# Row maxima and softmax denominators reach all partitions through DRAM instead of TensorE transposes, with exp four steps behind the scores

## The chip, the cores and the metric

The kernel runs on one NeuronCore of a Trainium2 chip. Its time is the device time of one execution in microseconds (us); lower is better. Five engines with instruction streams of their own matter here: TensorE (PE), VectorE (DVE), ScalarE (ACT), GpSimd (POOL) and SyncE (SP), which only issues DMAs. All five take their instructions in order, and wait on semaphores for each other.

## The reference

Four cross-attention layers run one after the other on `x` (2048 tokens, 256 channels), each with the same context (1601 rows of 512). Three layers are "masked" (16 heads of 64, a bias at a few keys from two masks), the second is "grouped" (16 query heads of 16 on 4 key heads, an RMS norm in front). All is float32. A masked layer, cut to what matters:

```python
q = (x @ Wq), k = (ctx @ Wk), v = (ctx @ Wv)          # 16 heads of 64
logits = einsum('bhqd,bhkd->bhqk', q, k) * 64 ** -0.5
logits = logits + col_bias                            # -20 * (1 - mask) at the token columns
probs = softmax(logits, axis=-1)                      # over 1601 keys
out = einsum('bhqk,bhkd->bhqd', probs, v)
x = x + out @ Wo + bo
```

The softmax of a query row needs the row's maximum before the exponential, and the row's sum afterwards.

## The kernel before, in words

Scores are kept transposed: keys on the 128 partitions, queries in the free dimension. A *unit* is two heads by 512 queries; a masked layer has 8 blocks (pairs of heads) by 4 query blocks, so 32 units, and there are 96 masked units and 32 grouped ones. The 1601 keys are 13 chunks of up to 128, so a unit has 13 *steps*. The main loop (L1067) runs over steps and overlaps three units in a software pipeline: at one step it makes the scores of chunk `ca` of one unit, the exponential of chunk `cb` of the unit before, `NT + DELAY` = 13 + 2 steps behind, and the product with V of the chunk one step (`LAG`) behind that.

A masked unit goes through these steps:

- `masked_scores` (L745): two matmuls into a PSUM buffer `s` (L751), ACT copies it to an SBUF chunk buffer `p` (L763), DVE keeps a running maximum `top` (L766, L768). The pool of `p` has `NP` = 17 buffers, that of `s` has two.
- `maxima` (L798), one step after the last chunk: eight TensorE transposes (L805) and a DVE reduction (L806) give the negative maximum `ntop`, one value per query, with the queries on the partitions.
- `maxima_spread` (L812), a step later: eight more transposes (L818) of a broadcast of `ntop` put the maxima on all partitions, in the PSUM buffer `b` named `less`.
- `subtract` (L831): DVE adds `less` to the chunk in place (L834). Then `exp` (L836): ACT takes the exponential in place (L841), and POOL adds the chunk to the running `sums` (L844 for chunks 0 and 1 together, L846 for the rest).
- `values` (L862): TensorE accumulates the product with V in `po` (L869); after the last chunk ACT copies it to `oT`.
- `denominators` (L881): eight transposes of `sums` (L888), a DVE reduction (L889) and a reciprocal (L890) give `rden`; POOL copies it in a broadcast form to `by` (L899).
- `divide` (L904): four transposes of `by` (L907) put the reciprocals on the partitions of the output, and DVE multiplies them into `o` (L911). `project` (L913): two matmuls with Wo (L917), each added to `xs` by DVE (L923).

The grouped units compute the maxima in another layout and fold them into a second matmul (L850, L855), get their denominators from a row of ones (L894, L897), and use the same L899, L907 and `project`. POOL makes no sums for them.

Between the scores and the values of a step, the loop puts *pieces* of other work into TensorE's stream: the projections of K (L369) and V (L384) for the next block, the queries of the next unit (L420), and denominators, divide and project of the unit just done. `Pieces` (L970) hands them out by a credit per step; `urgent` pieces go ahead of `fill`. The context slices `ct` that the projections read are loaded from DRAM by SP (L204), in three buffers, asked for as a piece starts.

At the end (L1125 to L1131) the instructions of PE, ACT and DVE are tied to the order in which they were written; those of POOL and SP are ordered by the framework's scheduler.

## Time and profile before

| | |
|---|---|
| median of 3 runs | 5643.22 us (5641.31 to 5643.86) |
| profiled execution | 5653.54 us, span 5651.8 us |
| granted TensorE clock, mean | 0.98 |
| PE, DVE, ACT, POOL busy | 94%, 71%, 57%, 50% of the span |
| DMA | 252.88 MB, mean 45 GB/s |

How to read it: a line such as `L846 POOL TENSOR_TENSOR sums<-sums,p 128x1024 f32<-128x1024 f32 (+1 forms) x1056 | 2499.2, 2367 | 1097.9 <-ACT p L841 1084.8` is a group of instructions of source line 846 on POOL: what is written from what, the shapes (partitions by elements), the count; then the busy time in us and the mean of one in ns; then how long the engine sat idle just before them, and which engine's work ended that. In the timeline a row has its start in us, its length in us, the engine, the line and the tiles; a bracket gives the idle time before it. TensorE's fp32 matmuls appear as two records each.

### The profile page before, as it was taken

The page shows a single profiled execution, that of the slowest core. Times are in us where ns is not written, and L with a number is a line of the kernel's source. Part 1 is how long each engine was busy: PE and PEld are TensorE (multiplying, and loading weights), DVE is VectorE, ACT ScalarE, POOL GpSimd, SP SyncE. Part 2 cuts the span into 40 slices and gives each one's busy share as a digit, 9 for nine tenths or more (in the row PEclk, how much of TensorE's full clock was granted, in tenths as well). Part 3 has the DMA queues.
Part 4 walks back from the last instruction along what each step waited for, and adds up shares of the span by engine and source line. Part 5 has one row for each costly group of instructions (what it writes and reads, how often), then busy time and mean ns, then how long its engine had stood idle before and what let it go on. Part 6 is the DMA issues. An engine that isn't in the chain of part 4 may idle for free.

```text
span 5651.8 us, 59516 instructions
## 1 busy us (share of the span) xinstructions
PE 5321.4 (94%) x22444; PEld 1865.2 (33%) x22444; DVE 4013.6 (71%) x4140; ACT 3196.2 (57%) x3513; POOL 2837.7 (50%) x1380
## 2 busy tenths in 40 slices
PE   6999999998889999999999999999999999999997
PEld 3333333332323333233233333333333333333332
DVE  3777777777765555555567777777777777777786
ACT  2666666665433434333456666666666666666665
POOL 1766666665410000000056666666666666666676
PEclk8999999999889999999999999999999999999998
DMA  4112211111100000001012111212111121111100
GB/s 135 32 57 60 59 49 53 55 56 44 39 20 5 9 9 9 9 13 52 15 51 61 56 54 49 57 56 59 46 56 55 54 59 49 53 56 52 54 17 15
DMA packets 209744, 252.88 MB, mean 45 GB/s; under 512 B 43529, under 2 KB 155401, under 8 KB 209456
## 3 DMA queue, kind: packets, MB, share of 16 engines
q1 hardware_dynamic: 206192, 243.69, 14.8%
q8 instruction: 177, 2.90, 0.2%
q0 software_dynamic: 1152, 3.28, 0.2%
q10 hardware_dynamic: 2112, 2.10, 0.1%
q14 instruction: 111, 0.91, 0.1%
HBM read 235.27 MB, written 13.76 MB: 44 GB/s over the span
## 4 chain that ended last, share of the span: by engine, by line
PE 78%; ACT 7%; POOL 7%; DVE 5%; issue 2%; DMA 0%; SPq 0%; ACTq 0%; POOLq 0%; DVEq 0%
PE po L869 24%; PE s L751 20%; PE pm L384 6%; PE pm L369 5%; PE pm L917 5%; POOL sums L844 4%; ACT p L763 4%; ACT p L841 3%; POOL sums L846 3%; PE s L850 2%; PE s L784 2%; PE pm L420 2%; PE s L805 2%; PE b L818 2%; PE s L855 2%
## 5 line engine op out<-in xcount | busy, mean ns | idle before, releaser
L846 POOL TENSOR_TENSOR sums<-sums,p 128x1024 f32<-128x1024 f32 (+1 forms) x1056 | 2499.2, 2367 | 1097.9 <-ACT p L841 1084.8
L763 ACT COPY p<-s 128x1024 f32<-128x1024 f32 (+1 forms) x1248 | 1263.4, 1012 | 1434.0 <-PE s L751 1138.3
L869 PE MATMUL po<-p,v 128*64 128x512 f32 (+1 forms) x6656 | 1821.7, 626 | 36.5 <-ACT p L841 34.7
L768 DVE TENSOR_TENSOR top<-s,top 128x1024 f32<-128x1024 f32 (+1 forms) x1056 | 1291.5, 1223 | 753.9 <-ACT p L763 749.4
L751 PE MATMUL s<-q,kT 64*128 64x512 f32 (+1 forms) x4992 | 1426.3, 648 | 117.6 <-DVE top L768 116.4
L834 DVE TENSOR_TENSOR p<-p,b 128x1024 f32<-128x1024 f32 (+1 forms) x1248 | 1504.7, 1206 | 2.4 <-PE b L818 2.0
L841 ACT ACTIVATE p<-p 128x1024 f32<-128x1024 f32 (+1 forms) x1248 | 1321.5, 1059 | 110.3 <-DVE p L834 109.4
L869 PEld LDWEIGHTS po<-p,v 128*64 128x64 f32 (+1 forms) x6656 | 332.0, 136 | 1032.1 <-issue 698.9
L899 POOL COPY by<-rden 128x512 f32<-128x512 f32 x128 | 78.5, 613 | 1111.8 <-DVE rden L897 1083.9
L751 PEld LDWEIGHTS s<-q,kT 64*128 64x128 f32 (+1 forms) x4992 | 370.7, 182 | 732.7 <-issue 454.6
L859 ACT ACTIVATE p<-s 128x1024 f32<-128x1024 f32 (+1 forms) x283 | 289.8, 1024 | 451.0 <-PE s L855 450.9
L844 POOL TENSOR_TENSOR sums<-p 128x1024 f32<-128x1024 f32 x96 | 226.5, 2360 | 434.2 <-ACT p L841 434.2
L789 DVE TENSOR_REDUCE row_top<-s 128x2 f32<-128x1024 f32 x261 | 318.6, 1221 | 122.9 <-PE s L784 121.9
L384 PEld LDWEIGHTS pm<-wv,ct 128*128 128x128 f32 (+1 forms) x2392 | 284.7, 187 | 218.9 <-issue 215.9
L384 PE MATMUL pm<-wv,ct 128*128 128x128 f32 (+1 forms) x2392 | 337.6, 286 | 0.5 <-ACT v L389 0.5
L369 PE MATMUL pm<-ct,wk 128*128 128x512 f32 (+1 forms) x736 | 315.8, 544 | 2.7 <-ACT kT L374 2.7
L917 PE MATMUL pm<-o,wo 128*128 128x512 f32 x512 | 292.0, 653 | 7.1 <-DVE xs L923 2.9
L859 ACT ACTIVATE p<-b 128x1024 f32<-128x1024 f32 (+1 forms) x133 | 136.2, 1024 | 217.8 <-PE b L855 217.8
L923 DVE TENSOR_TENSOR xs<-pm,xs 128x512 f32<-128x512 f32 x232 | 158.4, 683 | 90.4 <-PE pm L917 90.4
L806 DVE TENSOR_REDUCE ntop<-s 128x8 f32<-128x1024 f32 x96 | 117.6, 1225 | 130.9 <-PE s L805 130.6
L789 DVE TENSOR_REDUCE row_top<-b 128x2 f32<-128x1024 f32 x123 | 150.2, 1221 | 62.2 <-PE b L784 61.6
L420 PE MATMUL pm<-xT,wq 128*128 128x512 f32 x336 | 188.5, 644 | 0.0
(191 smaller groups left out, 3279.2 us busy)
## 6 DMA issues: line engine op xcount, KB each, us to landing
ct<-ctxT SPq DMA_DIRECT2D x288, 512.0 KB, 3.8
xT<-xT SPq DMA_DIRECT2D x104, 512.0 KB, 3.5
ct<-ctxT SPq DMA_DIRECT2D x48, 130.0 KB, 2.6
wk<-in_L_xattn_Wk_dram SPq DMA_DIRECT2D x24, 256.0 KB, 4.4
wv<-in_L_xattn_Wv_dram SPq DMA_DIRECT2D x24, 256.0 KB, 3.1
xT<-xs SPq DMA_DIRECT2D x12, 512.0 KB, 2.6
wq<-in_L_xattn_Wq_dram SPq DMA_DIRECT2D x24, 128.0 KB, 2.1
wo<-in_L_xattn_Wo_dram SPq DMA_DIRECT2D x24, 128.0 KB, 2.1
```

The costliest lines, as they stand in the source:

```text
L369: nc.tensor.matmul(u.pk[:, :n], u.wk[:, k, :], ct(k, a, n), start=(k == 0), stop=(k == NCT - 1),)
L384: nc.tensor.matmul(u.pv[:m, c - c0, :], ct(k, a, m), u.wv[:, k, :], start=(k == 0), stop=(k == NCT - 1),)
L751: nc.tensor.matmul(s[:m, h, :], self.u.kT[r, a : a + m], self.q[r, :], start=True, stop=(a != TAIL),)
L763: nc.scalar.copy(p[:m], s[:m])
L768: nc.vector.tensor_tensor(self.top[:m], s[:m], self.top[:m], ALU.max)
L789: nc.vector.tensor_reduce(self.top[:, :, q, k : k + 1], s, AX.X, ALU.max)
L834: nc.vector.tensor_tensor(self.p[c][:m], self.p[c][:m], self.less[:m], ALU.add)
L841: nc.scalar.activation(p[:m], p[:m], AF.Exp)
L844: nc.gpsimd.tensor_tensor(self.sums, self.p[0], p, ALU.add)
L846: nc.gpsimd.tensor_tensor(self.sums[:m], self.sums[:m], p[:m], ALU.add)
L869: nc.tensor.matmul(self.po[r, :], u.v[:m, c, r], self.p[c][:m, h, :], start=(c == 0), stop=(c == NT - 1),)
L917: nc.tensor.matmul(py, wo[:, ts(k, P)], self.o, start=True, stop=True)
```

## The change

- `maxima` of a masked unit sends `ntop` (128 partitions, 8 values) to a DRAM tile `cols` by one DMA, and a second DMA reads it back to all 128 partitions (512 KB) as `less`, now an SBUF tile. A query's values lie four apart in it, so `subtract` reads `less` with a step of 16 bytes. `maxima_spread` with its eight transposes is gone for masked units.
- `denominators` sends `rden` the same way, and two DMAs of 64 partitions read it back as `by`. `divide` multiplies `by` into `oT` in place; the POOL copy and the four transposes are gone, for masked and grouped units.
- The PSUM buffer `b` is given up for a third `s`. `NP` is 19, `DELAY` is 4. `wk`, `wv` and `xT` have one buffer instead of two.
- POOL starts `sums` with a copy of chunk 0 instead of adding chunks 0 and 1.
- The queries of the next unit come due two steps later, denominators two steps after the last values, divide and project four steps after that. The credit is no longer at least one piece per step. `ct` loads are asked for after the piece that frees their buffer.

```diff
-    NP = 17
+    NP = 19
-    ps_s = ctx.enter_context(tc.tile_pool(name="ps_s", bufs=2, space=PSUM))
-    ps_b = ctx.enter_context(tc.tile_pool(name="ps_b", bufs=1, space=PSUM))
+    ps_s = ctx.enter_context(tc.tile_pool(name="ps_s", bufs=3, space=PSUM))
...
+    def on_all_partitions(cols, to):
+        rows = dram.tile([2, P, QT], FP, name="cols", bufs=4)
+        with nc.allow_non_contiguous_dma(reason="1024 values, four at a time"):
+            nc.sync.dma_start(out=rows.rearrange("h p q -> p h q"), in_=cols)
+        for tile_, heads_ in to:
+            src = rows[heads_].rearrange("(o h) p q -> o (h p q)", o=1)
+            nc.sync.dma_start(out=tile_, in_=src.to_broadcast(tile_.shape))
...
                 nc.vector.tensor_reduce(ntop, pt, AX.X, ALU.max, negate=True)
+                less = work.tile([P, 2, P, QT], FP, name="less")
+                on_all_partitions(ntop, [(less.rearrange("n h p q -> n (h p q)"), slice(0, 2))])
+                self.less = less.rearrange("n h p q -> n h q p")
...
-                self.less = ps_b.tile([P, 2, QB], FP, name="b")
-                for h in range(2):
-                    for q in range(QT):
-                        nc.tensor.transpose(
-                            self.less[:, h, ts(q, P)],
-                            self.ntop[:, h, q : q + 1].to_broadcast((P, P)), ident,
-                        )
...
         def subtract(self, c):
             if self.masked:
                 m = TCH[c][1]
-                nc.vector.tensor_tensor(self.p[c][:m], self.p[c][:m], self.less[:m], ALU.add)
+                p = self.p[c][:m].rearrange("n h (q p) -> n h q p", p=P)
+                nc.vector.tensor_tensor(p, p, self.less[:m], ALU.add)
...
-                if c == 1:
+                if c == 0:
                     self.sums = work.tile([P, 2, QB], FP, name="sums")
-                    nc.gpsimd.tensor_tensor(self.sums, self.p[0], p, ALU.add)
-                elif c:
+                    nc.gpsimd.tensor_copy(self.sums, p)
+                else:
                     nc.gpsimd.tensor_tensor(self.sums[:m], self.sums[:m], p[:m], ALU.add)
...
-            self.by = work.tile([P, QT, 2, 64], FP, name="by", bufs=1)
-            nc.gpsimd.tensor_copy(
-                self.by,
-                rden.rearrange("p h (q o) -> p q h o", o=1).to_broadcast((P, QT, 2, 64)),
+            by = work.tile([P, P, QT], FP, name="by", bufs=1)
+            on_all_partitions(
+                rden,
+                [(by[self.rows(h)].rearrange("r p q -> r (p q)"), slice(h, h + 1)) for h in range(2)],
             )
+            self.by = by.rearrange("r p q -> r q p")
 
         def divide(self):
-            pr = ps_m.tile([P, QB], FP, name="pm")
-            for q in range(QT):
-                nc.tensor.transpose(
-                    pr[:, ts(q, P)], self.by[:, q].rearrange("p h o -> p (h o)"), ident
-                )
-            self.o = work.tile([P, QB], FP, name="o", bufs=1)
-            nc.vector.tensor_tensor(self.o, pr, self.oT, ALU.mult)
+            oT = self.oT.rearrange("r (q p) -> r q p", p=P)
+            nc.vector.tensor_tensor(oT, oT, self.by, ALU.mult)
+            return True
...
-            self.credit = min(self.credit + share, 2.0)
+            self.credit = min(self.credit, 0.9) + share
...
-    DELAY, LAG = 2, 1
+    DELAY, LAG = 4, 1
...
         if valuing and cv == NT - 1:
-            pieces.urgent.extend(valuing.finish_groups())
-            pieces.urgent.extend(after(kv))
+            due.setdefault(step + 2, []).append([valuing.denominators])
+            due.setdefault(step + 6, []).extend(valuing.finish_groups() + after(kv))
+        pieces.urgent.extend(due.pop(step, ()))
...
-            steps = NT - ca + (NT - 2) * after_this
-            pieces.step(max(1.0, (pieces.left() + 6 * after_this) / steps))
+            steps = NT - ca + (NT - 1) * after_this
+            pieces.step((pieces.left() + 5 * after_this) / steps)
```

## The prediction

> **What bounds the kernel now.** I read the page first: busy time, the chain, the costliest groups.
>
> ```profile
> PE 5321.4 (94%) x22444; PEld 1865.2 (33%) x22444; DVE 4013.6 (71%) x4140; ACT 3196.2 (57%) x3513; POOL 2837.7 (50%) x1380
> ...
> PE 78%; ACT 7%; POOL 7%; DVE 5%; issue 2%; DMA 0%; SPq 0%; ACTq 0%; POOLq 0%; DVEq 0%
> ...
> L846 POOL TENSOR_TENSOR sums<-sums,p 128x1024 f32<-128x1024 f32 (+1 forms) x1056 | 2499.2, 2367 | 1097.9 <-ACT p L841 1084.8
> ...
> L834 DVE TENSOR_TENSOR p<-p,b 128x1024 f32<-128x1024 f32 (+1 forms) x1248 | 1504.7, 1206 | 2.4 <-PE b L818 2.0
> L841 ACT ACTIVATE p<-p 128x1024 f32<-128x1024 f32 (+1 forms) x1248 | 1321.5, 1059 | 110.3 <-DVE p L834 109.4
> ```
>
> TensorE sets the pace; POOL's half share hides that it works only in the masked layers, 2.37 us per chunk. The chain in order of time gives TensorE's true pitch; two records are transposes that the change removes:
>
> ```profile
> 4200.65 1.06 PE s L751 x4
> 4201.72 1.01 PE po L869 x4
> 4202.72 1.02 PE b L818 x8
> ...
> 4256.55 0.66 PE pm L907 x4
> ```
>
> A masked unit on TensorE: 13 steps of 1.06 + 1.01 = 26.9; three sets of eight transposes (L805, L818, L888), 3.1; L907 0.7; four 512-wide matmuls (L420, L917) at 1.06 = 4.2; the bias 0.4; a quarter of a block's projections, (12 x 1.06 + 1.04 + 13 x 1.09) / 4 = 7.0. Sum 42.2 us. The window 4200 to 5500 holds 30 maxima reductions (L806), so a unit takes 43.3: TensorE idles 1.1.
>
> The decisive view is the timeline where DVE has an instruction with both inputs in SBUF while POOL adds a chunk. That happens only between layers:
>
> ```profile
> L691 DVE SCALAR_TENSOR_TENSOR xT<-xs,normw,rest x32: 337/349/2514, 1438.2 to 1637.6; 128x128 f32<-128x128 f32 x32
> ```
> ```profile
> 1442.00 1.97 DVE L691 SCALAR_TENSOR_TENSOR xT<-xs,normw,rest 128x128 f32<-128x128 f32 x2
> ...
> 1449.98 0.61 DVE L691 SCALAR_TENSOR_TENSOR xT<-xs,normw,rest 128x128 f32<-128x128 f32 x2
> ```
> ```profile
> 1441.20 2.35 POOL L846 TENSOR_TENSOR sums<-sums,p 128x1024 f32<-128x1024 f32 x1 [3.44 <-ACT p L841]
> 1446.33 2.35 POOL L846 TENSOR_TENSOR sums<-sums,p 128x1024 f32<-128x1024 f32 x1 [2.77 <-ACT p L841]
> ```
>
> The pair at 1449.98, with no sum beside it, takes 0.61. The pair at 1442.00 takes 1.97: POOL's sum ends at 1443.55, and the pair ends 0.42 later. DVE stands still until POOL is done. L834 shows nothing of this today (always near 1206 ns): its second input `b` lies in PSUM.
>
> **What the change removes.** From TensorE, per masked unit 1.02 + 0.66 = 1.7 us, leaving 40.5; per grouped unit 0.66. From POOL the copy L899 (128 of 0.61). The wait of ACT for POOL's first sum, which comes of adding chunks 0 and 1 together, goes with the copy of chunk 0; what it cost is within the 1.1. Late next is not TensorE:
>
> **What it adds, 1: two engines on one port.** `less` moves to SBUF, so all 13 subtractions of a masked unit become what L691 is, beside a POOL that sums in the same steps. In series a unit needs 12 sums x 2.37 = 28.4, the copy of chunk 0 about 1.0 (L899 does half the elements in 0.61, the rest by POOL's other rows), 13 subtractions x 1.21 = 15.7, and a divide of 0.69, also two SBUF inputs now: 45.9. A blocked DVE instruction has its start behind it when the port comes free; the cast L523 ended 0.29 after POOL where alone it takes 0.42, so 0.13 is hidden, 1.7 a unit: 44.2. Were POOL's start hidden too, 42.5. The trace never shows DVE first and POOL waiting; the ends are 0 (they overlap) and 1.21 a chunk. I take the full exclusion, the nearest row being the exclusion seen from the other side.
>
> To reach 44.2 POOL must have a sum waiting whenever DVE lets go. `NP` 19 allows about two steps of lag (13 + 4 + 2). But DVE's stream puts other work between two subtractions: the denominators' reduction and reciprocal in one step, divide and a residual add in another. There POOL goes first, DVE loses its turn, and the port then waits for an exp (1.06 and some 0.17 of handoffs). Two such turns a unit: 2.4. Masked unit: 46.6, against 43.3: +3.3 x 96 = **+317 us**.
>
> **2: round trips in place of transposes.** A trip is a 4 KB write of 16-byte pieces and a read on all partitions. Rows for landing times:
>
> ```profile
> xT<-xT SPq DMA_DIRECT2D x104, 512.0 KB, 3.5
> ...
> wq<-in_L_xattn_Wq_dram SPq DMA_DIRECT2D x24, 128.0 KB, 2.1
> ...
> wo<-in_L_xattn_wo_dram SPq DMA_DIRECT2D x16, 16.0 KB, 1.7
> ...
> tok_idx<-ttn_token_indices_A_dram SPq DMA_DIRECT2D x3, 1.0 KB, 3.2
> ```
>
> The write lies between 1.7 and 3.2; I take 1.9, nearer the short row, as it spreads over all partitions. Reads of `by` are two of 128 KB in flight together, 2.1 (4.4 at worst, as wk's 256 KB). With 0.4 of issues and handoffs, 4.4 us, from 3.8 to 8.0.
>
> For `less` it is 1.9 + 3.5 + 0.4 = 5.8. In DVE's stream three subtractions and three maxima stand between the reduction and the first use, about 10 us: nothing, unless SP is held in front of it by a context load waiting for TensorE (such waits last up to 24 us today); then the subtraction waits, with every maximum behind it.
>
> For `by` there is less cover than the diff suggests. Divide comes due four steps after denominators, but the credit, no longer one per step, hands denominators out late and divide promptly. In the built program DVE has 3, 2 or 1 pairs of subtraction and maximum between reciprocal and divide in masked units (0 in three). At 3.4 us a pair only the last kind (21 units, 1.0 short) waits; it drains POOL's backlog meanwhile, so I charge nothing more; uncovered, it would be 0.2 a unit on average.
>
> Grouped units have no slack: their TensorE is 98% busy (1700 to 2650: 934.25 of 950). From the denominator matmuls to project: handoffs and reciprocal 0.4, trip 4.4, divide 0.69, handoffs 0.4, so 5.9. TensorE's stream holds between them nothing in nine units, 2.1 to 2.4 us in seventeen, 4.8 in three, 11 or more in three: 9 x 5.9 + 17 x 3.5 + 3 x 1.1 = 116 us of stall, less 32 x 0.66 of transposes, +95. A gap that long also costs clock:
>
> ```profile
> 1446.24 1.08 PE L869 MATMUL po<-p,v 128*64 128x512 f32 x4 [2.99 <-ACT p L841]
> ...
> 1452.87 1.98 PE L869 MATMUL po<-p,v 128*64 128x512 f32 x4 [3.31 <-ACT p L841]
> ```
>
> After 2.99 idle the four records take 1.08, after 3.31 idle 1.98, and it stays so until 1462.3: some 4.7 us lost. For the nine with the longest gap, +42. Together **+137**. With trips of 3.8 and no clock loss +75; with 8.0, and clock lost at 29 gaps, some +330.
>
> **3: the rest, at nothing.** The third `s` was there in grouped units as `b`; in masked ones it only lets scores run further ahead. Single `wk`, `wv`: their loads (4.4, 3.1 us) come after the last projection of a block, and SP's stream has them among the work of the last steps; the first projection that needs them comes a step or more later. If late, once per block: 24 x 4.4 = 105 at most. Moved `ct` loads go past `cols` in SP's stream in 22 of 128 denominators; the next piece bounds that. Some 85 MB more DMA on 253 MB at 15% of the queues: no bound. The last unit's trip at the end: +6.
>
> **The step of 16 bytes.** Here a row and a rule differ. `subtract` reads one element in four. The nearest row is a DVE copy read at a step of 64 bytes (L273), beside one without a step (L251):
>
> ```profile
> L273 DVE COPY max_cols<-p x8: 170/174/181, 91.5 to 98.0; 128x24 f32<-128x24 f32 x8
> ```
> ```profile
> L251 DVE COPY max_cols<-less x32: 174/174/176, 1586.3 to 2779.9; 128x8 f32<-128x8 f32 x32
> ```
>
> Twenty-four stepped elements take the same 174 ns as eight dense ones, so I take no loss. But the row is short. DVE's rows for 512 elements show two rates a factor apart, 0.42 us (L523) and 0.69 (L524), a start of 0.15 taken off: 1 to 2; one more halving is the other end, 13 x 1.07 + 0.53 = +14.4 a unit. The Trainium skill (Advanced Engine Details and Errata, Memory Cachelines) says that SBUF lines are 16 bytes and that at least two accesses to a line are needed to hide its latency; at this step each access meets a new line. By the row the total is the sum below; by the rule, taken as a halved rate, it would be about 7480 (an estimate).
>
> **Sum**, against the profiled execution of 5653.5 (span 5651.8): 5653.5 + 317 + 137 + 6 = 6114. It lies 10 above the median of the runs, so about **6100** in their terms.
>
> **Rivals.**
> - *The step halves the rate.* Subtraction 2.28: +14.4 x 96 = 1382 more, 7480. For: no row reads 1024 elements at a step. Against: L273.
> - *Lock step.* If POOL never has a sum waiting, a chunk is subtraction 1.08, exp 1.06, sum 2.37, handoffs 0.17: 4.7, a unit 13 x 4.7 - 1.3 + 0.7 = 60.5, and 7440 in all; half the steps so, about 6770. For: subtraction and exp feed the very sum that blocks the next subtraction. Against: after its maximum DVE asks for the port some 0.1 us before the exp is done.
> - *Faster: no exclusion* between this add and the sums, since `tensor_tensor` itself was never seen blocked. Then TensorE stays the bound: 40.5, plus its stall at project, where the chain from the denominators' transposes is 5.9 + 1.5 = 7.4 against covers of 8.5, 4.2, 5.3 and 2.1 in a block's four units: 2.6 on average. 43.1 a unit, -20, and the grouped 137: 5770. With a trip of 3.4 (two landings of 1.7) the stalls shrink to 1.8 and 2.8: (42.3 - 43.3) x 96 + 69 + 6 = -21, 5622. It decides from a trip below about 4.0. Against: L691 and L523 are blocked each time a sum runs.
>
> **How the numbers follow.** Exclusion with unit 44.2 to 48.5 and grouped +75 to +330: 0.48, 5810 to 6480, the forecast 6100. Lock step, partly or whole: 0.17. Halved rate: 0.15. No exclusion with the usual trip: 0.08, of which 0.03 within 0.2%. With the short trip, faster: 0.12. A measurement tells 0.2% (11 us) from no change. Faster 0.12, same 0.03, slower 0.85. The range 5660 to 7460 leaves out the faster cases and the upper end of the slowest.
>
> **What would show it.** Subtractions well over 1.21 us wherever a sum runs, ending just after it, or POOL's sums longer; a masked unit of 46 to 47; TensorE near 87% with the longest waits on DVE; in grouped units waits at project on the divide, the divide on a DMA, and a lower granted clock there. I am wrong if subtraction stays at 1.21 beside a sum of 2.37, or if it is 2.3 with no sum beside it.

## The result, and the profile after

The changed kernel takes **7425.75 us** (median of four runs, 7423.34 to 7426.9), the kernel before 5643.54 beside it (5641.31 to 5646.77). The ratio is 1.3157, with a 95% interval from 1.3134 to 1.318. The forecast was 6100: the direction was right and the time lies inside the stated range, 5660 to 7460, but near its upper end: the loss is 1782 us, where some 456 had been forecast.

From the page of the kernel after (span 7421.6): busy times, the chain that ended last, and four of the costliest groups.

```profile
PE 5643.3 (76%) x21164; PEld 1831.4 (25%) x21164; DVE 6154.7 (83%) x4140; ACT 3240.7 (44%) x3513; POOL 4540.9 (61%) x1348
...
DVE 35%; PE 29%; issue 28%; DMA 5%; ACT 1%; POOL 1%; SPq 0%; DVEq 0%; POOLq 0%; ACTq 0%
...
L855 POOL TENSOR_TENSOR sums<-sums,p 128x1024 f32<-128x1024 f32 (+1 forms) x1152 | 4241.1, 3682 | 1286.1 <-ACT p L850 1076.9
L843 DVE TENSOR_TENSOR p<-p,less 128x1024 f32<-128x1024 f32 (+1 forms) x1248 | 3569.3, 2861 | 2.4 <-DMA less<-cols 2.2
...
L923 PE MATMUL pm<-oT,wo 128*128 128x512 f32 x512 | 437.3, 949 | 666.5 <-DVE oT L916 602.9
...
L916 DVE TENSOR_TENSOR oT<-oT,by 128x512 f32<-128x512 f32 x128 | 239.0, 1867 | 173.7 <-DMA by<-cols 173.7
```

TensorE has 1280 matmul records fewer, and yet more busy time than before: its granted clock is 0.89, where it was 0.98. DVE is the busiest engine. Its subtraction has gone from 1.21 to 2.86 us, POOL's sum from 2.37 to 3.68. Both records hold waiting inside them, as the timeline of a masked stretch shows (start, length, engine, line; POOL's five sums are one row):

```profile
5017.63 18.88 POOL L855 TENSOR_TENSOR sums<-sums,p 128x1024 f32<-128x1024 f32 x5 [0.33 <-ACT p L850]
...
5020.50 3.10 DVE L843 TENSOR_TENSOR p<-p,less 128x1024 f32<-128x1024 f32 x1
...
5023.51 1.22 DVE L782 TENSOR_TENSOR top<-s,top 128x1024 f32<-128x1024 f32 x1
...
5024.64 3.05 DVE L843 TENSOR_TENSOR p<-p,less 128x1024 f32<-128x1024 f32 x1
...
5027.62 1.21 DVE L782 TENSOR_TENSOR top<-s,top 128x1024 f32<-128x1024 f32 x1
...
5028.75 3.11 DVE L843 TENSOR_TENSOR p<-p,less 128x1024 f32<-128x1024 f32 x1
...
5034.28 4.07 DVE L843 TENSOR_TENSOR p<-p,less 128x1024 f32<-128x1024 f32 x1
...
5041.19 1.64 DVE L916 TENSOR_TENSOR oT<-oT,by 128x512 f32<-128x512 f32 x1 [1.71 <-DMA by<-cols]
```

A subtraction follows a maximum every 4.1 us, while POOL's sums run without a pause. At 5034.28, after the denominators' reduction and reciprocal, DVE comes 0.11 us behind POOL's next sum (start 5034.17) and stands until it is over. At 5041.19 the divide has waited for its DMA.

Where did the 1782 us go? The start of the maxima's reduction on DVE marks the masked units. The mean distance of its 94 successive starts inside the masked layers is a masked unit; the one long distance spans the grouped layer. Before: 44.31 us and 1293.7. After: 60.16 and 1553.4. So 15.85 x 96 = 1522 lie in the masked units and 260 in the grouped stage: 1782.

### The profile page after: what moved, and what is told of

Same layout as the page of the kernel before. It is cut to its first block, busy times and chain, and to the rows that moved or that the text cites. A ratio compares the mean times of both kernels' runs of the same rounds, so it can differ in the third digit from the quotient of the medians.

```text
span 7421.6 us, 57991 instructions
## 1 busy us (share of the span) xinstructions
PE 5643.3 (76%) x21164; PEld 1831.4 (25%) x21164; DVE 6154.7 (83%) x4140; ACT 3240.7 (44%) x3513; POOL 4540.9 (61%) x1348
## 3 DMA queue, kind: packets, MB, share of 16 engines
q0 software_dynamic: 1152, 3.28, 0.1%
## 4 chain that ended last, share of the span: by engine, by line
DVE 35%; PE 29%; issue 28%; DMA 5%; ACT 1%; POOL 1%; SPq 0%; DVEq 0%; POOLq 0%; ACTq 0%
DVE top L782 14%; DVE p L843 12%; PE po L878 7%; PE pm L923 6%; PE s L765 4%; DVE oT L916 3%; DMA by<-cols 3%; PE s L798 3%; PE s L859 2%; DMA cols<-rden 2%; PE s L864 2%; PE pm L370 2%; DVE rden L898 1%; DVE top L780 1%; DVE ntop L820 1%
## 5 line engine op out<-in xcount | busy, mean ns | idle before, releaser
L855 POOL TENSOR_TENSOR sums<-sums,p 128x1024 f32<-128x1024 f32 (+1 forms) x1152 | 4241.1, 3682 | 1286.1 <-ACT p L850 1076.9
L843 DVE TENSOR_TENSOR p<-p,less 128x1024 f32<-128x1024 f32 (+1 forms) x1248 | 3569.3, 2861 | 2.4 <-DMA less<-cols 2.2
L878 PE MATMUL po<-p,v 128*64 128x512 f32 (+1 forms) x6656 | 1946.4, 665 | 1006.3 <-ACT p L850 890.0
L765 PE MATMUL s<-q,kT 64*128 64x512 f32 (+1 forms) x4992 | 1532.1, 693 | 0.7 <-DVE top L780 0.7
L923 PE MATMUL pm<-oT,wo 128*128 128x512 f32 x512 | 437.3, 949 | 666.5 <-DVE oT L916 602.9
L868 ACT ACTIVATE p<-s 128x1024 f32<-128x1024 f32 (+1 forms) x416 | 425.6, 1023 | 882.6 <-PE s L864 881.9
L853 POOL COPY sums<-p 128x1024 f32<-128x1024 f32 x96 | 267.2, 2784 | 735.5 <-ACT p L850 735.5
L803 DVE TENSOR_REDUCE row_top<-s 128x2 f32<-128x1024 f32 x384 | 469.0, 1224 | 218.6 <-PE s L798 215.1
L916 DVE TENSOR_TENSOR oT<-oT,by 128x512 f32<-128x512 f32 x128 | 239.0, 1867 | 173.7 <-DMA by<-cols 173.7
L859 PE MATMUL s<-q,kT 128*128 128x512 bf16 (+1 forms) x832 | 259.3, 395 | 4.4 <-DVE row_top L803 2.3
L798 PE MATMUL s<-kT,q 128*128 128x512 bf16 (+1 forms) x1024 | 259.4, 353 | 0.2 <-ACT p L868 0.2
```

What stands on the lines that cost most here:

```text
L765: nc.tensor.matmul(s[:m, h, :], self.u.kT[r, a : a + m], self.q[r, :], start=True, stop=(a != TAIL),)
L798: nc.tensor.matmul(s[:, h, at : at + n], self.q8[:, h, ts(q, P)], self.u.k8[:, a : a + n], start=True, stop=True,)
L803: nc.vector.tensor_reduce(self.top[:, :, q, k : k + 1], s, AX.X, ALU.max)
L843: nc.vector.tensor_tensor(p, p, self.less[:m], ALU.add)
L855: nc.gpsimd.tensor_tensor(self.sums[:m], self.sums[:m], p[:m], ALU.add)
L878: nc.tensor.matmul(self.po[r, :], u.v[:m, c, r], self.p[c][:m, h, :], start=(c == 0), stop=(c == NT - 1),)
```

## The experiments

The theory after reading the trace: the step of 16 bytes lengthens the subtraction, and since DVE and POOL lock each other out, it lengthens the series that both form on what the prediction calls the port (the way to SBUF on which a sum of POOL and a DVE instruction with two SBUF inputs take turns); the round trips are a second, smaller loss. The rivals: lock step by itself, the exclusion by itself, the trips and the new order of steps by themselves. All runs in one table, by the two measures above. An interval is that of the ratio to the kernel before, run beside it; below the first two rows, a time without one is of a single execution.

| run | time, us | masked unit | grouped distance |
|---|---|---|---|
| before | 5643.54 | 44.31 | 1293.7 |
| after | 7425.75 | 60.16 | 1553.4 |
| after, rows of `cols` dense | 7896.38 | 62.64 | 1795.3 |
| after, no sums | 6405.68 | 49.85 | 1532.1 |
| after, dense and no sums | 7779.06 | 61.58 | 1786.2 |
| after, `less` copied to PSUM | 6448.69 | 49.96 | 1561.5 |
| after, `less` copied to dense SBUF | 6859.93 | 54.47 | 1539.6 |
| after, denominators at their step | 7144.29 | 59.37 | 1351.1 |
| the same, `less` copied to dense SBUF | 6492.46 | 52.72 | 1336.2 |
| the same, `less` copied to PSUM | 6002.48 (1.0638, 1.0621 to 1.0656) | 47.52 | 1341.7 |
| the same, divide a step ahead | 5684.96 (1.007, 1.0053 to 1.0087) | 44.28 | 1328.2 |
| before, `less` copied to dense SBUF | 6225.85 | 50.28 | 1305.6 |
| before, `less` copied to stepped SBUF | 7339.46 | 61.87 | 1316.9 |
| before, chunk 0 copied | 5536.69 (0.9808, 0.9791 to 0.9824) | 43.19 | 1293.8 |
| the same, 19 buffers | 5534.4 (0.9809, 0.9792 to 0.9825) | 43.11 | 1293.6 |
| the same (17 buffers), denominators by DRAM | 5573.56 (0.9875, 0.9859 to 0.9892) | 43.07 | 1333.6 |

### Step and exclusion in the changed kernel

A dense layout, written by the DMA itself:

```diff
-        rows = dram.tile([2, P, QT], FP, name="cols", bufs=4)
+        rows = dram.tile([2, QT, P], FP, name="cols", bufs=4)
-            nc.sync.dma_start(out=rows.rearrange("h p q -> p h q"), in_=cols)
+            nc.sync.dma_start(out=rows.rearrange("h q p -> p h q"), in_=cols)
...
-                less = work.tile([P, 2, P, QT], FP, name="less")
+                less = work.tile([P, 2, QT, P], FP, name="less")
...
-            by = work.tile([P, P, QT], FP, name="by", bufs=1)
+            by = work.tile([P, QT, P], FP, name="by", bufs=1)
```

> The changed kernel with the rows of `cols` written head, part, position instead of head, position, part, so that `less` and `by` lie dense and the subtraction and the divide read them without a step; everything else as changed. Theory (a step of 16 bytes slows the subtraction from 1.21 to 1.92 us, and beside that it shares a port with POOL's sums): an undisturbed subtraction falls back to 1.2 us, the port's series from 55.5 to 45.9 us a masked unit, the unit from 59.7 to 47 to 50 us, the whole to 6200 to 6500 us. Rival (subtraction, exp and sum run in lock step, whatever the step costs): a unit stays near 60 and the whole above 7200. Rival (the exclusion is nothing, the step alone makes DVE the bound): a unit near 43, the whole near 5850.

It took 7896.38 us with 62.64 a unit, which by the numbers is the first rival's band (lock step), but for another reason: the edit brought a cost of its own. DMA issues of the changed kernel, and of this one (count, size, median us from issue to landing):

```profile
cols<-rden SPq DMA_DIRECT2D x128, 4.0 KB, 1.9
```
```profile
cols<-rden SPq DMA_DIRECT2D x128, 4.0 KB, 10.0
```

The same 4 KB in pieces of 4 bytes land after 10.0 us, in pieces of 16 after 1.9. The trip is 8 us longer, and both `less` and `by` come late (DVE waits 502 us for the one and 1085 for the other). So the run decides nothing on the step or on lock step, but shows what a longer trip costs.

The sums left out, with the step kept:

```diff
                 if c == 0:
                     self.sums = work.tile([P, 2, QB], FP, name="sums")
-                    nc.gpsimd.tensor_copy(self.sums, p)
-                else:
-                    nc.gpsimd.tensor_tensor(self.sums[:m], self.sums[:m], p[:m], ALU.add)
+                    nc.gpsimd.memset(self.sums, 1.0)
```

> The changed kernel without POOL's sums: it fills `sums` with ones once a unit instead of adding up the 13 chunks, so the denominators are left out; the step of 16 bytes stays. Theory: the subtraction is 1.92 us everywhere, DVE has about 13 x 1.92 + 12 x 1.22 + 5 = 45 to 46 us a masked unit and is the bound; the whole is 6050 to 6200 us. Rival (the exclusion is nothing): nothing changes, the subtraction keeps its mean of 2.84 and the whole stays near 7400. Rival (the round trips and the order of the steps cost most): above 6800.

6405.68 us. This run shows the step by itself. The subtraction's durations (shortest, median, longest in ns) with nothing on POOL, and in the kernel before:

```profile
L843 DVE TENSOR_TENSOR p<-p,less x1248: 1912/2045/2237, 124.5 to 6375.3; 128x1024 f32<-128x1024 f32 x166, 65x1024 f32<-65x1024 f32 x13
```
```profile
L834 DVE TENSOR_TENSOR p<-p,b x1248: 1167/1209/1222, 134.6 to 5619.3; 128x1024 f32<-128x1024 f32 x166, 65x1024 f32<-65x1024 f32 x13
```

Without company it takes 2.045 us with the step, where it took 1.209: 0.836 more, a factor of 1.69. The time came out above the band all the same. DVE is only 79% busy and not the bound: TensorE's projections waited 539 us for the divide. The trips, then, cost more than the theory had it as soon as POOL leaves the port free.

Both edits together:

> Both at once: dense `less` and `by`, and no sums (the denominators are left out, `sums` is filled with ones). What is left of the slow-down is the round trips and the order of the steps. Theory: subtraction 1.21, DVE 37 us a masked unit, TensorE at 40.5 to 43 us, and the 260 us that the grouped stage lost stay: 5750 to 5950 us. Rival (trips and order cost most): above 6500. Rival (trips cost nothing when DVE is quick): 5400 to 5600.

7779.06 us, the first rival's band, against 7896.38 with the sums: with a write of 10 us the trip outweighs the rest, and whether POOL sums or not moves the time by 1.5%.

So the layout was made dense in another way, by ScalarE, once a unit. Into PSUM (two `s` buffers and `b`, as before), or into SBUF:

```diff
+                if c == 0:
+                    b = ps_b.tile([P, 2, QT, P], FP, name="b")
+                    nc.scalar.copy(b, self.less)
+                    self.less = b
```

```diff
+                if c == 0:
+                    dense = work.tile([P, 2, QT, P], FP, name="dense", bufs=1)
+                    nc.scalar.copy(dense, self.less)
+                    self.less = dense
```

> The changed kernel with its round trips and its order of steps, but ScalarE copies `less`, still laid out with the step, into a PSUM buffer without a step once a unit, and the subtraction reads that; `s` has two buffers again. This takes away the step and the exclusion together and leaves the sums. Theory: subtraction 1.2 us beside sums of 2.37, a masked unit of 43 to 45 us, the 260 us of the grouped stage and a wait at project stay: 5750 to 6000 us. Rival (trips and order cost most): above 6500. Rival (the loss is all in the subtraction): 5450 to 5650.

6448.69 us: without step and exclusion 977 of the 1782 us are gone, and 805 stay. The theory's band was missed by 450. Subtraction and sums are back at 1.21 and 2.37, so what stays does not lie in them; the longest wait of TensorE is the projection for the divide, 621.3 us, as in the changed kernel (602.9). The run adds a cost of its own: DVE waits 190.9 us in all for ScalarE's copy.

```profile
L848 DVE TENSOR_TENSOR p<-p,b 128x1024 f32<-128x1024 f32 (+1 forms) x1248 | 1506.2, 1208 | 191.1 <-ACT b L845 190.9
L928 PE MATMUL pm<-oT,wo 128*128 128x512 f32 x512 | 444.7, 965 | 684.2 <-DVE oT L921 621.3
```

> The changed kernel, but once a unit ScalarE copies the stepped `less` into a dense SBUF tile, and the subtraction reads that (`less` has one buffer): the exclusion without the step. With the copy into PSUM, which takes away both, it was 6448.7 us, with both 7425.8. Theory (step and exclusion matter together, since both lengthen the port's series): the subtraction is 1.2 us undisturbed, near 2 on average beside the sums; the series of 46 us lies under the some 49 us that a masked unit took with the PSUM copy, so the whole is 6450 to 6750 us. Rival (exclusion alone is the loss): above 7000. Rival (the step alone is the loss): within 30 us of 6448.7.

6859.93 us, between the bands: exclusion alone adds 411 to the PSUM copy, and the step another 566. DVE's wait for ScalarE's copy (193.6 us here) is in both copied runs and not in the changed kernel, so the step is probably worth more than this difference. Neither is the whole loss.

### The trip of `by`

In the changed kernel's stream TensorE has between a unit's denominators and its projection the values of no, one or two chunks in 67 of 96 masked units, and of none or one in 26 of 32 grouped ones, since denominators wait for a credit and the divide does not. Here they are issued at their step (grouped ones after the piece in hand):

```diff
-            due.setdefault(step + 2, []).append([valuing.denominators])
+            ending[step + 2] = valuing
...
+        if step in ending:
+            if not ending[step].masked:
+                pieces.flush()
+            ending.pop(step).denominators()
```

Now at least four chunks lie between, in all but one unit.

> The changed kernel, but a unit's denominators are issued at their step itself instead of waiting in the queue of pieces for a credit, so TensorE's stream holds at least four steps of values between them and the projection (it was one or two in most masked units and none or one in grouped ones); step and exclusion stay. Theory (the round trip of `by` stands uncovered in every unit, some 800 us of the loss, and the port's series of 54 to 56 us a masked unit is the rest): the wait of the projection for the divide falls from 603 to under 100 us, the grouped stage comes back to the time before, the whole is 6600 to 7000 us. Rival (the trip is covered in masked units by DVE's backlog, as the prediction had it, and only the grouped 260 us go): 7100 to 7200. Rival (nothing of it is the trip): above 7350.

7144.29 us: the first rival's band. Of the 281 us gained 202 are the grouped stage's; a masked unit gains 0.8. While the port sets the pace, the trip is nearly hidden in a masked unit, and the grouped stage pays for it.

This edit and the PSUM copy together:

> Both cures together: `less` copied into PSUM by ScalarE, and denominators issued at their step. Theory (step with exclusion, and the uncovered trip, are the whole loss): TensorE is the bound again with 40.5 us of work a masked unit and without 0.66 us of transposes in a grouped one; 5480 to 5700 us. Rival (the order of steps with a delay of four, three quarters of a pair of `s` buffers or the cleared credit costs by itself): 5750 to 6200. Rival (the copy on ScalarE and DVE's wait for it are a new bound): above 6200, with DVE's wait for `b` over 300 us.

6002.48 us, in the first rival's band, and 446 less than with the late denominators: what was hidden behind the port is bare without it. But 360 us above the kernel before (5642.27 beside it) are left. The timeline shows where (L921 is the divide, L928 the projection, L766 the scores):

```profile
4934.91 1.21 DVE L848 TENSOR_TENSOR p<-p,b 128x1024 f32<-128x1024 f32 x1
...
4936.03 1.22 DVE L783 TENSOR_TENSOR top<-s,top 128x1024 f32<-128x1024 f32 x1
...
4937.17 1.06 DVE L921 TENSOR_TENSOR oT<-oT,by 128x512 f32<-128x512 f32 x1
...
4938.37 1.76 PE L928 MATMUL pm<-oT,wo 128*128 128x512 f32 x2 [2.55 <-DVE oT L921]
4940.06 2.08 PE L766 MATMUL s<-q,kT 64*128 64x512 f32 x4
```

The DMA is long in. The divide still stands directly in front of the projection, behind a subtraction and a maximum; TensorE waits 2.55 us for it, and its next records run at about half speed. So the divide was issued a step ahead, and the copy into PSUM a step earlier (grouped denominators, too, come a step sooner):

```diff
+            ending[step + 5] = valuing.divide
             due.setdefault(step + 6, []).extend(valuing.finish_groups() + after(kv))
...
-            return [[self.divide]] + [[lambda k=k: self.project(k)] for k in range(NC)]
+            return [[lambda k=k: self.project(k)] for k in range(NC)]
```

> As the run with the PSUM copy and denominators issued at their step, with two handoffs drawn apart: the divide is issued a step ahead of the projection (it stood directly in front of it, behind the step's subtraction and maximum on DVE), and ScalarE copies `less` into PSUM at the end of the step before the first subtraction. Theory (the 360 us that were left there are the divide's own stretch in front of the projection, 315 us of waiting and the lower clock behind it, and the copy's handoffs): TensorE waits under 60 us at the projection, its clock is 0.98 or more, a masked unit takes 41 to 42 us; 5380 to 5580 us. Rival (the delay of four and the cleared credit cost by themselves): 5750 to 6000. Rival (ScalarE's copy of 2 us is the new bound): 5600 to 5800, with DVE's wait for `b` still over 150 us.

5684.96 us. The projection and the subtraction, without and with this edit:

```profile
L928 PE MATMUL pm<-oT,wo 128*128 128x512 f32 x512 | 341.4, 753 | 346.1 <-DVE oT L921 314.8
L848 DVE TENSOR_TENSOR p<-p,b 128x1024 f32<-128x1024 f32 (+1 forms) x1248 | 1506.8, 1208 | 187.9 <-ACT b L845 185.2
```
```profile
L929 PE MATMUL pm<-oT,wo 128*128 128x512 f32 x512 | 298.1, 665 | 102.4 <-DVE xs L935 45.7
L849 DVE TENSOR_TENSOR p<-p,b 128x1024 f32<-128x1024 f32 (+1 forms) x1248 | 1505.8, 1207 | 173.5 <-ACT b L842 173.4
```

The wait for the divide fell from 314.8 to 27.4 us, the clock is 0.979, and 317 of the 360 us are gone: they were handoffs, not the delay of four. DVE's wait for the copy hardly moved (185.2 to 173.4), so most of the gain is the divide's. The time is in the second rival's band, though, not in the theory's: DVE still waits for ScalarE's copy, which takes 2.03 us. With the trips covered and a subtraction that has neither step nor exclusion (the divide keeps both), the changed kernel is 0.7% slower than the kernel before.

### Step and exclusion in the kernel before

Here no trip and no order is changed. ScalarE copies the transposed maxima out of PSUM, dense (`[P, 2, QT, P]`) or with the step (`[P, 2, P, QT]`):

```diff
+                less = work.tile([P, 2, QT, P], FP, name="less", bufs=1)
+                less = less.rearrange("n h q p -> n h q p")
+                nc.scalar.copy(less, self.less.rearrange("n h (q p) -> n h q p", p=P))
+                self.less = less
```

> The kernel before with one thing done: ScalarE copies the spread maxima from PSUM into a dense SBUF tile once a unit, and the subtraction reads that. No trip, no step, no other order: the exclusion alone. The prediction's term for this was a masked unit of 44.2 us in series and 46.6 with two lost turns, against 43.3: 5650 to 5970 us. Theory now (the two engines lock each other out as predicted): 5750 to 6050, the subtraction near 2 us on average, POOL's sums lengthened too. Rival (no exclusion): 5640 to 5700, the subtraction at 1.21. Rival (lock step): above 6300.

6225.85 us, between the theory's band and lock step's: the exclusion costs 6.0 us a masked unit, near twice the 3.3 of the prediction. DVE's wait for ScalarE's copy, 76.5 us in all or 0.8 a unit, is in it. POOL's sums (L851) and the subtraction (L839) over the whole run, first with the dense copy, then with the stepped one of the next run:

```profile
L851 POOL TENSOR_TENSOR sums<-sums,p 128x1024 f32<-128x1024 f32 (+1 forms) x1056 | 3061.9, 2899 | 1046.5 <-ACT p L846 994.9
L839 DVE TENSOR_TENSOR p<-p,less 128x1024 f32<-128x1024 f32 (+1 forms) x1248 | 2677.6, 2146 | 84.3 <-ACT less L824 76.5
```
```profile
L851 POOL TENSOR_TENSOR sums<-sums,p 128x1024 f32<-128x1024 f32 (+1 forms) x1056 | 3512.8, 3327 | 1256.3 <-ACT p L846 1204.3
L839 DVE TENSOR_TENSOR p<-p,less 128x1024 f32<-128x1024 f32 (+1 forms) x1248 | 3649.8, 2925 | 190.2 <-ACT less L824 190.1
```

From the timeline of a masked stretch of the dense run (on DVE L768 is the maximum, L916 the divide; L926, the residual addition, lies in the rows left out):

```profile
4531.93 2.35 POOL L851 TENSOR_TENSOR sums<-sums,p 128x1024 f32<-128x1024 f32 x1 [0.77 <-ACT p L846]
4532.01 0.69 DVE L916 TENSOR_TENSOR o<-pm,oT 128x512 f32<-128x512 f32 x1 [0.18 <-PE pm L912]
4532.61 2.74 DVE L839 TENSOR_TENSOR p<-p,less 128x1024 f32<-128x1024 f32 x1
4535.28 1.21 DVE L768 TENSOR_TENSOR top<-s,top 128x1024 f32<-128x1024 f32 x1
4535.39 1.06 ACT L846 ACTIVATE p<-p 128x1024 f32<-128x1024 f32 x1 [0.30 <-DVE p L839]
...
4536.59 2.36 POOL L851 TENSOR_TENSOR sums<-sums,p 128x1024 f32<-128x1024 f32 x1 [2.31 <-ACT p L846]
...
4541.26 2.35 POOL L851 TENSOR_TENSOR sums<-sums,p 128x1024 f32<-128x1024 f32 x1 [2.32 <-ACT p L846]
...
4545.76 1.21 DVE L839 TENSOR_TENSOR p<-p,less 128x1024 f32<-128x1024 f32 x1
4545.93 6.55 POOL L851 TENSOR_TENSOR sums<-sums,p 128x1024 f32<-128x1024 f32 x2 [2.32 <-ACT p L846]
```

Two regimes alternate. From 4531.93 to 4545.93 a sum starts every 4.67 us: lock step. Each time here a small instruction (a divide, then L926 at 4536.63 and 4541.08) puts DVE's subtraction behind the start of POOL's sum, the subtraction waits the sum out, the exponential waits for the subtraction, and the next sum for the exponential. At 4545.76 nothing stood in between, DVE came 0.17 us ahead of POOL, and the next two sums take 6.55 us, 3.28 each. Both regimes were in the prediction, as forecast and as rival; the kernel runs in both in turn. Over the whole trace, 534 sums start 3.31 us (median) after the one before and 345 start 4.67 us after it, so a masked unit has 5.6 of the one and 3.6 of the other.

> The same with the SBUF tile laid out as in the change, so that the subtraction reads it with a step of 16 bytes: step and exclusion without any trip. Theory (the port's series grows from 46 to some 54 to 58 us a masked unit): 6550 to 7100 us, the subtraction 1.92 us at its shortest and near 2.8 on average. Rival (the step costs nothing by itself once POOL excludes DVE anyway): within 100 us of the dense run. Rival (TensorE's uncovered trips are what made the changed kernel slow): under 6200.

7339.46 us, above the theory's band and within 87 of the whole change, without any trip. The step costs 11.6 us a masked unit in this order; 1.2 of them are DVE's longer wait for ScalarE's copy (190.1 us in all, 76.5 in the dense run), which itself takes twice as long when it writes with the step. Both regimes are as frequent as in the dense run and longer: 4.14 us 540 times, and lock step 5.43 us 346 times, as here (sums at 5061.40, 5066.85, 5072.27):

```profile
5061.40 2.35 POOL L851 TENSOR_TENSOR sums<-sums,p 128x1024 f32<-128x1024 f32 x1 [0.76 <-ACT p L846]
5066.85 2.35 POOL L851 TENSOR_TENSOR sums<-sums,p 128x1024 f32<-128x1024 f32 x1 [3.10 <-ACT p L846]
5072.27 2.35 POOL L851 TENSOR_TENSOR sums<-sums,p 128x1024 f32<-128x1024 f32 x1 [3.07 <-ACT p L846]
```

Does the change's own order, with its longer delay and its buffers, keep the engines out of lock step? The run is the changed kernel with denominators at their step and `less` copied to dense SBUF:

> The changed kernel with denominators issued at their step (the trip covered) and with ScalarE's copy of `less` into a dense SBUF tile: the exclusion alone, in the change's order of steps. In the order before it cost 6.0 us a masked unit (50.3 against 44.3). Theory (two more chunk buffers, a delay of four and the copied chunk 0 give POOL the backlog that keeps the two engines out of lock step, as the prediction had it): a masked unit of 46.5 to 48.5 us, 5930 to 6130 us. Rival (the order gives no relief, DVE loses its turns as before): 49.5 to 52 us a unit, 6220 to 6460. Rival (the order makes it worse): above 6500.

6492.46 us and 52.72 a unit, above the first rival's band: the time shows no relief. Against the same kernel with the PSUM copy (47.52) the exclusion costs 5.2 us, near the 6.0 in the order before; both have ScalarE's copy in them, for which DVE waits 2.0 us a unit. Sums in lock step stand 4.67 us apart here as well, but there are fewer of them: 212, or 2.2 a unit, where the order before had 3.6. So the order does keep the engines out of lock step more often, but the unit's time shows nothing of it; the projection's wait for the divide, 366.1 us in this run, stands against it.

### What of the change is worth keeping

```diff
-                if c == 1:
+                if c == 0:
                     self.sums = work.tile([P, 2, QB], FP, name="sums")
-                    nc.gpsimd.tensor_tensor(self.sums, self.p[0], p, ALU.add)
-                elif c:
+                    nc.gpsimd.tensor_copy(self.sums, p)
+                else:
```

> The kernel before with one part of the change alone: POOL copies chunk 0 into `sums` and adds chunk 1, where it added chunks 0 and 1 in one. ScalarE's copy of scores waited 174 us in all for a chunk buffer that the first sum held. Theory (TensorE sets the pace and that wait is mostly hidden): within 30 us of the time before, 5610 to 5655. Rival (that wait is on the path): 5480 to 5600. Rival (1.0 us more of POOL a unit matters): 5660 to 5750.

5536.69 us, 1.9% faster than before. TensorE's waits for the running maximum, before and with the copy (us in total, times, longest):

```profile
PE s L751 <- DVE top L768: 116.4, 71, 2.7
```
```profile
PE s L751 <- DVE top L768: 29.8, 71, 1.9
```

Chunk 0's buffer was held until chunk 1 had been through the exponential and the first sum. ScalarE's copy of scores waited for it (174.5 us, now 58.6), DVE's maximum for that copy, and TensorE for the `s` buffer. The gain is 1.12 us a masked unit.

On top of it the change's chunk buffers and single weight buffers (`wv` and the grouped layer's `wk` and `wv` are edited like the `wk` shown):

```diff
-    NP = 17
+    NP = 19
...
-            u.wk = weights.tile([P, NCT, P], FP, name="wk")
+            u.wk = weights.tile([P, NCT, P], FP, name="wk", bufs=1)
```

> The kernel before with POOL's copy of chunk 0, and with the change's 19 chunk buffers and single `wk` and `wv`. Theory (with the copy, ScalarE hardly waits for chunk buffers any more and TensorE is busy for 96%): 5520 to 5545 us, no different from 5536.7. Rival (more buffers let ScalarE's copies run further ahead): 5450 to 5515. Rival (the single weight buffers hold a block's first projections up): 5550 to 5650.

5534.4 us: no difference beside 5536.69. And on top of the copy, with 17 buffers, the change's way of the denominators and its divide, each issued at a step of its own:

```diff
-            pieces.urgent.extend(valuing.finish_groups())
-            pieces.urgent.extend(after(kv))
+            ending[step + (2 if valuing.masked else 1)] = valuing.denominators
+            ending[step + 5] = valuing.divide
+            due[step + 6] = valuing.finish_groups() + after(kv)
```

> The kernel before with POOL's copy of chunk 0 and with one more part of the change: denominators go through DRAM, issued one or two steps after the last values, with the divide at the fifth step and the projection at the sixth; maxima stay with the transposes and `less` in PSUM. Theory (a trip with four steps of cover costs nothing, and the transposes of the denominators, 128 x 0.66 = 84 us, leave a TensorE that sets the pace): 5450 to 5530 us, against 5536.7 with the copy alone. Rival (the divide, now with two SBUF inputs behind POOL's sums, or a lower clock takes it back): 5530 to 5650. Rival (a trip cannot be hidden): above 5700.

5573.56 us, 37 more, although 84 us of transposes are gone: the first rival's band. In masked units the projection waits for the divide (120 of the run's 121.7 us), which takes 2.60 us on average, since it has two SBUF inputs now and stands behind POOL's sums; that takes back most of what the transposes gave, and the unit is as long as with the copy alone (43.07 beside 43.19). The loss lies in the grouped stage, where POOL makes no sums and the divide takes 1.18 us: its distance grew by 40 us. TensorE there is idle for 22 us more, in many short waits, and busy for 17 us more with 131 records fewer, at a granted clock of 0.97 in place of 0.99.

## Why the prediction was right in sign and wrong in size

**The step that failed: "The step of 16 bytes".** It took no loss, since 24 stepped elements cost 174 ns like 8 dense ones. The row was too short: 1024 elements cost 2.045 us in place of 1.209, the divide 1.06 in place of 0.69. By a unit that is 13 x 0.836 + 0.37 = 11.2 us on the port, nothing in the forecast's sum. The Trainium skill (Advanced Engine Details and Errata, Memory Cachelines) says that going to a new 16-byte line with each access brings a penalty, and this case agrees: a factor of 1.69, below the halved rate that the rival assumed. The mechanism by which it counts was in the prediction: it lengthens the port's series. With POOL silent the run with the step was no slower than the run with the PSUM copy, which has neither step nor exclusion (6405.68 and 6448.69, though the second also pays for ScalarE's copy); with POOL's sums the step cost 11.6 us a unit in the order before. In the changed kernel, taking the step away gave back less, 5.7 us a unit (6.7 with the trip covered), since ScalarE's copy cost DVE 2.0 and the waits for the divide stayed.

**Exclusion: right in kind.** The subtraction does wait out a sum that came first, and POOL waits out a subtraction that came first (its record grows from 2.37 to 4.05 at the median), which the trace of before could not show. The Trainium skill (SBUF — State Buffer, SBUF: two separate sides) calls the pair "an **exclusive lock**, not a bandwidth split", held for the whole instruction; both records agree.

**Two lost turns per unit, 2.4 us: right in number, but not all that is lost.** In the changed kernel 737 of 1152 sums start 4.14 us (median) after the one before and 189 start 5.43 us after it: two lost turns a unit, of 1.3 us each. The rival of lock step was partly right: lock step sets in where a small instruction stands in front of DVE's subtraction, and in the kernel before with an SBUF operand it holds over several chunks. The base was mis-sized the other way: a chunk takes 4.14 us where 2.045 + 2.37 - 0.13 makes 4.28, and 3.31 without the step where the prediction has 3.45, so more than 0.13 is hidden behind each wait. With the measured step the prediction's series would be 44.2 + 11.2 = 55.4 us. In the run with the trip covered the records of sums, subtractions and divides cover only 53.8 of the 59.37 us of a unit; for 5.6 us the port is idle, 3.2 more than the lost turns explain. What fills the rest wasn't taken apart.

**`by` in masked units, charged nothing: nearly right.** It costs 0.8 us. But the reason holds only while the port is the bound; without it, the late denominators and the handoffs of divide and copy cost 49.96 - 44.28 = 5.7 us.

In the prediction's terms the masked unit is 44.2 + 11.2 for the series, 4.0 for all turns and waits (59.37 - 55.4) and 0.8 for `by`: 60.2, measured 60.16, predicted 46.6. The sum closes because its last two terms are differences of measured units. The unit before was a little off as well: 43.3 in the window that was read, 44.31 over all units. The rivals of the halved rate (7480) and of lock step (7440) both come within 1% of the measured time, by luck: the first has a step of 14.4 us in place of 11.2, the second has no step at all, and both take the forecast's 137 us for the grouped stage.

**Grouped units: +260, predicted +137.** `by` lands 3.2 us after its issue, where 2.1 was taken from `wq`'s row, and the clock fell throughout: 0.90 in the stretch from 2500 to 3300, where the prediction let it fall behind the longest gaps only. TensorE is idle there for 197 us more than before (predicted: 116), and busy for 62 us more with 154 records fewer. With the trip covered the stage is at +57.

**What was taken at nothing:** `less` is hidden (2.2 us of waiting in the whole run), single `wk` and `wv` together with 19 chunk buffers cost nothing (5534.4 beside 5536.69), and the wait for POOL's first sum, put at no more than 1.1 us a unit, was worth 1.12. This last was the one part of the change that paid by itself among those tried, and the prediction named it without pricing it as a gain.

**Left open:** what makes the grouped stage 40 us longer in the run with denominators by DRAM, its short waits or the clock behind them, was not tried apart, and ScalarE's copy of 2.03 us was not replaced by a dense one, so whether the maxima's trip could pay in a kernel without that wait isn't shown.

## What to carry to other kernels

Before moving an operand from PSUM to SBUF, add up what DVE and POOL then do in series on their shared port, with the operand's real stride, and compare that sum with the bound: here some 54 us of port against 42 of TensorE. A round trip needs its cover in the stream of the engine that waits at its end, and the last handoff in front of that engine (here a divide directly before its matmul) wants a step of its own. Try a change's parts one by one: one small edit out of this one was worth 1.9%, inside a whole that cost nearly 32%.

## What was not expected of the hardware

- A 4 KB write to DRAM takes 10.0 us in 1024 pieces of 4 bytes and 1.9 us in 256 pieces of 16 (median landing).
- The step costs ScalarE more than DVE: a copy of 128x1024 from PSUM to SBUF takes 1.01 us dense and 2.02 us when it writes with a step of 16 bytes, and a copy from SBUF to PSUM that reads with this step takes 2.03 us; DVE's add goes from 1.21 to 2.05. ScalarE's copies in the kernel before, dense and stepped (shortest, median, longest in ns):

```profile
L824 ACT COPY less<-b x96: 987/1012/1012, 123.6 to 6157.6; 128x1024 f32<-128x1024 f32 x96
```
```profile
L824 ACT COPY less<-b x96: 1985/2017/2047, 123.6 to 7259.0; 128x1024 f32<-128x1024 f32 x96
```

- A broadcast read of two times 128 KB (`by`) lands after 3.2 us, one of 512 KB (`less`) after 3.8: twice the bytes in all, 0.6 us more.
